# One list of evenly cut projection pieces for a whole attention program, v by halves, and the softmax sums in the accumulator's bank

## The chip, the cores and the metric

The kernel runs on one core of a Trainium2 chip. The metric is the time of one execution on the device in microseconds (us). The engines that matter are TensorE (PE, matrix products; its weight loads are shown apart as PEld), ScalarE (ACT, here only the exponential), VectorE (DVE), GpSimd (POOL) and the queue of SyncE (SP), which issues most transfers.

## What is computed

A batch of four images with 512 channels and 48x48 = 2304 positions goes through group normalisation, eight-head attention with a head size of 64, an output projection and a residual sum:

```python
hn = _group_norm(x, scale, bias)
qkv = jnp.einsum('oc,bchw->bohw', qkv_w, hn) + qkv_b[None, :, None, None]
qkv = qkv.reshape(b, 3, num_heads, d, t).astype(jnp.float16)
q, k, v = (qkv[:, 0], qkv[:, 1], qkv[:, 2])
scale = jnp.asarray(1.0 / math.sqrt(math.sqrt(d)), dtype=jnp.float16)
w = jnp.einsum('bhct,bhcs->bhts', q * scale, k * scale)
w = jax.nn.softmax(w, axis=-1)
a = jnp.einsum('bhts,bhcs->bhct', w, v).astype(jnp.float32)
a = a.reshape(b, c, hh, ww)
out = jnp.einsum('oc,bchw->bohw', proj_w, a) + proj_b[None, :, None, None]
return x + out
```

## The kernel before

`fast_path` does all the work here; `general_path` follows only if a flag says that some softmax sum left a safe range. Heads are taken in pairs: four batches of four pairs make 16 pairs `g` (`NG`). The 2304 query positions of a pair are cut into five blocks `j`, four of 512 and one of 256 (`QBLOCKS`). Keys come in 18 tiles of 128. A **step** (one entry of `stream`) handles three groups of two score tiles: six steps for a block of 512, three for the block of 256, 27 for a pair (`per_pair`), 432 in all.

In one step, `scores` (L784) multiplies k by q into one of three double banks `ps` of PSUM, and ScalarE takes the exponential of each into `p` (L803). One step later `values` (L806) multiplies v by `p` into the single accumulator bank `av`, and `add` (L841) sums the `p` tiles of the block on VectorE into `acc`. After the last step of a block VectorE copies `av` out (`avx`, L829). `add_up` (L855) multiplies `acc` by ones, which gives the softmax sums `sl`; VectorE copies them to `slx` (L872), a transfer puts them on partitions (`sums`), VectorE inverts them (L888), and two more transfers through DRAM (`row`, `ib`) spread the inverse; `divide` (L878) multiplies on GpSimd into `att`.

Beside the steps stands the **projection work** that feeds TensorE in between: q and k of later pairs (`qk_chain`, L641), v of the next batch (`v_chain`, L681), the output projection of the last batch (`proj_chain`, L730, with the weights split in a high and a low part), loading, statistics and normalisation of the next batch's x. A chain is a row of matmuls that ends in one bank; all chains, the group means and also `sl` use the one bank `pw` (`chain_bank`, L576), so a chain can start only when VectorE has emptied the one before. Chains are listed as pieces, one for each of the four channel chunks `c`, with an assumed length in us. Each batch has a list of its own (`beside[b]`); `fill` (L998) issues pieces until the batch's list is as far along as the batch's steps are. In the step in which `add_up` runs there is no `fill` (L1032 to L1035), since `sl` needs the bank `pw`; and the step before closes an open chain for the same reason.

The order on TensorE and VectorE is the order of the program; the other queues are ordered by the framework. Before the first step TensorE computes, with nothing beside it, q and k of pair 0 and all of v of batch 0 (L977 to L985): 10 chains for q and k, and 18 for v with 512 columns each. Behind the last step stands what is left of the last batch's projection, and the count of safe sums (L1040 to L1044).

Of the kernel before, what the change touches and what calls it, by code (L numbers as in the profile page):

```python
# [25 lines left out]
P = 128  # L26
# [439 lines left out]
def fast_path(  # L466
# [18 lines left out]
    apool = ctx.enter_context(tc.tile_pool(name="apool", bufs=6))  # L485
# [149 lines left out]
    def piece(us, run, first=False, last=False):  # L635
        return [us, run, first, last, 0, NG]
# [4 lines left out]
    def qk_chain(g, part, j):  # L641
# [4 lines left out]
        def one(c):  # L646
# [26 lines left out]
        return [  # L673
            piece(n / 600.0, lambda c=c: one(c), c == 0, c == NC - 1)
            for c in range(NC)
        ]
# [4 lines left out]
    def v_chain(b, i):  # L681
        pw = {}
        at = i * P % QB

        def one(c):
            if i == 0 and c == 0:
                vv[b] = [
                    vpool.tile(
                        [P, NT, C // 2], F16, tag=f"v{a}", bufs=1 + a, name=f"v{a}_{b}"
                    )  # L690
                    for a in range(2)
                ]
            if c == 0:
                pw[0] = chain_bank(f"pv_{b}_{i}")
            for lo in (0, D):
                nc.tensor.matmul(  # L696
                    pw[0][lo : lo + D, :],
                    hn[b, c, i * P // QB][:, at + lo : at + lo + D],
                    wqkv[:, c, 2 * C :],
                    start=(c == 0),  # L700
                    stop=(c == NC - 1),
                )
            if c == NC - 1:
                for half in range(2):
                    cols = bass.ts(half, C // 2)
                    nc.vector.tensor_tensor(  # L706
                        vv[b][half][:, i, :], pw[0][:, cols], bv[:, cols], ALU.add
                    )

        return [  # L710
            piece(0.86, lambda c=c: one(c), c == 0, c == NC - 1) for c in range(NC)
        ]
# [10 lines left out]
    def att32(b, j):  # L723
        o, n = QBLOCKS[j]
        t = work.tile([P, NC, QB], F32R, tag="a32", bufs=1, name=f"a32_{b}_{j}")
        for c in range(NC):
            nc.gpsimd.tensor_copy(t[:, c, :n], atts[b * NPAIR + c][:, o : o + n])  # L727
        at32[b, j] = t

    def proj_chain(b, j, m):  # L730
        o, n = QBLOCKS[j]
        ps = chain_bank(f"pr_{b}_{j}_{m}")
        for c in range(NC):
            for i, w in enumerate((whi, wlo)):
                nc.tensor.matmul(  # L735
                    ps[:, :n],
                    w[:, c, bass.ts(m, P)],
                    at32[b, j][:, c, :n],
                    start=(c == 0 and i == 0),
                    stop=(c == NC - 1 and i == 1),  # L740
                )
        xt = res.pop((b, j, m))
# [5 lines left out]
    def proj_block(b, j):  # L748

        pieces = []  # L750

        def ahead(k):
            if k < NQ * NC:
                pieces.append(piece(0.0, lambda: residual(b, k // NC, k % NC)))

        if j == 0:
            ahead(0)
            ahead(1)
        pieces.append(piece(0.0, lambda: att32(b, j)))
        for m in range(NC):  # L760
            ahead(j * NC + m + 2)
            pieces.append(
                piece(
                    QBLOCKS[j][1] / 290.0,
                    lambda m=m: proj_chain(b, j, m),
                    True,
                    True,
                )
            )
        return pieces  # L770
# [3 lines left out]
    av, acc, pts, avx, sums = {}, {}, {}, {}, {}  # L774
# [31 lines left out]
    def values(u):  # L806
# [3 lines left out]
        per = QB // n  # L810
        if k == 0:
            if j == 0:
                new_att(g)
            av[0] = ps_av.tile([P, QB], F32, tag="av", name=f"av_{g}_{j}")
        for r in range(BURST):
            for a in range(per):
                i = (k * BURST + r) * per + a
                for h in range(2):
# [3 lines left out]
                        vv[b][pr // 2][:, i, pr % 2 * P + lo : pr % 2 * P + lo + D],  # L822
                        pts[u][:, r, h, a * n : (a + 1) * n],
# [7 lines left out]
    def new_att(g):  # L831
        if g >= NG - 2:

            if g == NG - 2:
                spare = vpool.tile([P, 2, T], F16, tag="v1", bufs=2, name="att_last")
                for i in range(2):
                    atts[g + i] = spare[:, i, :]
        else:
            atts[g] = apool.tile([P, T], F16, tag="att", name=f"att_{g}")

    def add(u):  # L841

        g, j, k, _ = u
        pt = pts.pop(u)
        if k == 0:
            acc[g, j] = pt
            return
        before = acc[g, j]
        if k == 1:
            acc[g, j] = work.tile(  # L850
                [P, BURST, 2, QB], F16, tag="acc", bufs=1, name=f"acc_{g}_{j}"
            )
        nc.vector.tensor_tensor(acc[g, j], before, pt, ALU.add)  # L853

    def add_up(g, j):  # L855
        o, n = QBLOCKS[j]
        per = QB // n
        sl = chain_bank(f"sl_{g}_{j}")
        t = acc.pop((g, j))
        steps = [(r, a) for r in range(BURST) for a in range(per)]  # L860
        for r, a in steps:
            for h in range(2):
# [5 lines left out]
                    start=((r, a) == steps[0]),  # L868
                    stop=((r, a) == steps[-1]),
                )  # L870
        sx = work.tile([P, QB], F32, tag="rows", name=f"slx_{g}_{j}")
        nc.vector.tensor_copy(sx[:, :n], sl[:, :n])  # L872

        sums[g, j] = small.tile([P, 2, QB // P], F32, tag="sums", name=f"sums_{g}_{j}")
        for h in range(2):
            nc.sync.dma_start(sums[g, j][:, h, : n // P], sx[h * D : h * D + 1, :n])

    def divide(g, j):  # L878
        o, n = QBLOCKS[j]
        per = n // P  # L880
        sm = sums.pop((g, j))[:, :, :per]
        ok = fine[:, :, :per]
        for op, limit in ((ALU.is_ge, SUM_MIN), (ALU.is_le, SUM_MAX)):
            t = small.tile([P, 2, QB // P], F32, tag="in", name=f"in_{g}_{j}")
            nc.gpsimd.tensor_scalar(t[:, :, :per], sm, limit, None, op)  # L885
            nc.gpsimd.tensor_tensor(ok, ok, t[:, :, :per], ALU.mult)
        inv = small.tile([P, 2, QB // P], F32, tag="inv", name=f"inv_{g}_{j}")
        nc.vector.reciprocal(inv[:, :, :per], sm)  # L888
# [3 lines left out]
        )  # L892
        ib = work.tile([P, QB], F32, tag="rows", name=f"ib_{g}_{j}")
# [9 lines left out]
    beside = {b: [] for b in range(B)}  # L903

    def put(b, pieces, after=0, need=NG):
        for p in pieces:
            p[4], p[5] = after, need
        beside[b] += pieces

    def put_qk(b, g, parts, after=0):  # L910
        for part in parts:
            for j in range(NQ):
                put(b, qk_chain(g, part, j), after, g)

    for b in range(B):
        g = b * NPAIR
        if b == 0:
            for j in range(NQ):
                if j < NC:
                    put(b, [piece(0.0, lambda c=j: load_wproj(c))])  # L920
                if j > 0:
                    put(b, [piece(0.0, lambda c=j - 1: split_wproj(c))])
                for part in (1, 0):
                    put(b, qk_chain(g + 1, part, j), 0, g + 1)
        else:
            put_qk(b, g + 1, (0,))
        put_qk(b, g + 2, (1, 0))
        if b == B - 1:
            put(b, proj_block(b - 1, 0))
            put_qk(b, g + 3, (1, 0), per_pair - 1)  # L930
# [168 lines left out]
```

## Time and profile before

| | |
|---|---|
| time, median of 3 runs | 1798.94 us (1796.32 to 1800.29) |
| the profiled execution | 1798.37 us, of which its span is 1796.6 us |
| ScalarE busy | 1220.1 us, 68% of the span |
| VectorE busy | 1030.8 us, 57% |
| GpSimd busy | 334.7 us, 19% |
| moved to and from memory | 82.15 MB, mean 46 GB/s |

The span reaches from the first to the last instruction of the profiled execution; the 1.8 us around it are in the time and not in the profile. "Busy" is the time in which an engine had at least one instruction under way; the profile's ends of matmuls are modelled. In the views, L803 is line 803 of the kernel, `out<-in` are the program's names with the buffer numbers left out, and an arrow in brackets names what ended a wait.

### The profile page before, as it was taken

Reading aid. Unit: us, or ns where it says so; the run is one execution under the profiler, and the core shown is the slowest. Engines: PE = TensorE matmul, PEld = TensorE weight load, DVE = VectorE, ACT = ScalarE, POOL = GpSimd, SP = SyncE. Lnnn points to the kernel's source line nnn. Section 1 sums busy time; section 2 is a strip of 40 time slices with the busy share of each in tenths; the row PEclk is TensorE's granted clock in tenths of the full one; section 3 lists DMA queues with packets and bytes.
Section 4 is the critical chain, followed back from the end, with each engine's and each line's share of the span. In section 5 each row is a group of like instructions: output and inputs, shape, how many; then the busy total and the mean of one; then the engine's idle time right before and its main releaser. Section 6 shows DMA issues by size and latency. Waiting matters only on the chain. (4 is left out here: it accounts for less than half of the span.)

```text
span 1796.6 us, 26704 instructions
## 1 busy us (share of the span) xinstructions
PE 1652.7 (92%) x10706; PEld 649.1 (36%) x10706; DVE 1030.8 (57%) x1194; ACT 1220.1 (68%) x1297; POOL 334.7 (19%) x561
## 2 busy tenths in 40 slices
PE   4999997999999989899999998989999999999885
PEld 1333332333333343433333344343333334334443
DVE  5226557656555555756455555675555566666663
ACT  0027776677787775866677777685667888887971
POOL 1000122111121123210011113231011111222331
PEclk9999999999999999999999999999999999999998
DMA  5001022000000043310000014330000001104233
GB/s 194 0 1 31 19 50 78 10 13 13 10 14 16 17 112 118 90 39 13 10 13 16 13 40 122 107 92 13 13 10 13 14 15 23 53 16 132 61 107 110
DMA packets 90406, 82.15 MB, mean 46 GB/s; under 512 B 51488, under 2 KB 58144, under 8 KB 90272
## 3 DMA queue, kind: packets, MB, share of 16 engines
q1 hardware_dynamic: 83712, 62.75, 12.9%
q0 software_dynamic: 4592, 14.18, 2.7%
q10 hardware_dynamic: 1968, 3.41, 0.6%
q8 instruction: 86, 1.41, 0.3%
q14 instruction: 48, 0.39, 0.1%
HBM read 60.83 MB, written 19.17 MB: 45 GB/s over the span
## 5 line engine op out<-in xcount | busy, mean ns | idle before, releaser
L803 ACT ACTIVATE p<-ps 128x1024 f16<-128x1024 f32 x1296 | 1218.8, 1038 | 523.6 <-PE ps L796 523.4
L655 PE MATMUL pqk<-x,wqkv 128*64 128x512 f32 (+1 forms) x2560 | 530.4, 551 | 6.4 <-DVE x L628 4.4
L853 DVE TENSOR_TENSOR acc<-acc,p 128x3072 f16<-128x3072 f16 x272 | 482.3, 1773 | 31.0 <-ACT p L803 29.5
L796 PE MATMUL ps<-q,k 64*128 64x512 f16 (+1 forms) x2880 | 388.2, 360 | 64.0 <-ACT p L803 63.1
L820 PE MATMUL av<-p,v 128*64 128x512 f16 (+1 forms) x2880 | 363.7, 366 | 0.6 <-DVE avx L829 0.6
L655 PEld LDWEIGHTS pqk<-x,wqkv 128*64 128x64 f32 x2560 | 179.4, 137 | 255.3 <-issue 196.7
L796 PEld LDWEIGHTS <-k 64*128 64x128 f16 x2880 | 119.3, 94 | 412.3 <-issue 366.9
L696 PE MATMUL pv<-wqkv,x 128*64 128x512 f32 x1152 | 260.7, 599 | 4.3 <-DVE x L628 4.3
L885 POOL TENSOR_SCALAR in<-sums 128x8 f32<-128x8 f32 (+1 forms) x160 | 55.1, 345 | 964.3 <-DMA sums<-slx 957.9
L820 PEld LDWEIGHTS <-v 128*64 128x64 f16 x2880 | 125.6, 109 | 188.9 <-issue 149.6
L898 POOL TENSOR_TENSOR att<-avx,ib 128x512 f16<-128x512 f32 (+1 forms) x70 | 105.6, 1508 | 303.4 <-DMA ib<-row 275.9
L853 DVE TENSOR_TENSOR acc<-p,p 128x3072 f16<-128x3072 f16 x80 | 145.1, 1814 | 24.8 <-ACT p L803 24.7
L735 PE MATMUL pr<-a,whi 128*128 128x512 f32 (+1 forms) x320 | 126.1, 401 | 19.2 <-DVE r L743 10.3
L706 DVE TENSOR_TENSOR v<-pv,bv 128x256 f16<-128x256 f32 x144 | 54.4, 420 | 144.1 <-PE pv L696 144.0
L696 PEld LDWEIGHTS pv<-wqkv,x 128*64 128x64 f32 x1152 | 81.3, 138 | 148.2 <-issue 131.3
L664 DVE TENSOR_SCALAR k<-pqk,bqkv 128x512 f16<-128x512 f32 (+1 forms) x80 | 55.7, 696 | 109.4 <-PE pqk L655 109.4
L735 PE MATMUL pr<-a,wlo 128*128 128x512 f32 (+1 forms) x320 | 117.6, 374 | 0.0
L664 DVE TENSOR_SCALAR q<-pqk,bqkv 128x512 f16<-128x512 f32 (+1 forms) x80 | 55.6, 696 | 105.1 <-PE pqk L655 105.1
L829 DVE COPY avx<-av 128x512 f32<-128x512 f32 (+1 forms) x80 | 51.0, 637 | 92.9 <-PE av L820 92.0
L872 DVE COPY slx<-sl 128x512 f32<-128x512 f32 (+1 forms) x80 | 51.0, 637 | 86.2 <-PE sl L864 85.9
L743 DVE SCALAR_TENSOR_TENSOR r<-pr,bproj,r 128x512 f32<-128x512 f32 (+1 forms) x80 | 55.4, 693 | 47.6 <-PE pr L735 37.8
L735 PEld LDWEIGHTS pr<-a,whi 128*128 128x128 f32 x320 | 60.1, 188 | 59.1 <-issue 19.5
(48 smaller groups left out, 456.3 us busy)
## 6 DMA issues: line engine op xcount, KB each, us to landing
r<-x_dram SPq DMA_DIRECT2D x64, 256.0 KB, 2.9
ib<-row SPq DMA_DIRECT2D x128, 128.0 KB, 3.1
out_dram<-r SPq DMA_DIRECT2D x64, 256.0 KB, 3.0
x<-x_dram POOLq DMA_DIRECT2D x48, 256.0 KB, 3.3
x<-x_dram ACTq DMA_DIRECT2D x8, 256.0 KB, 7.0
x<-x_dram SPq DMA_DIRECT2D x8, 256.0 KB, 7.0
wqkv<-qkv_wT_dram SPq DMA_DIRECT2D x2, 1024.0 KB, 8.2
sums<-slx SPq DMA_DIRECT2D x128, 2.0 KB, 2.0
```

The source lines that it names most:

```text
L655: nc.tensor.matmul(pw[0][lo : lo + D, :n], wqkv[:, c, w0 + lo : w0 + lo + D], hn[b, c, j], start=(c == 0), stop=(c == NC - 1),)
L664: nc.vector.tensor_scalar(qk[g][part][:, o : o + n], pw[0][:, :n], bqkv[:, col : col + 1], SCALE, ALU.add, ALU.mult,)
L696: nc.tensor.matmul(pw[0][lo : lo + D, :], hn[b, c, i * P // QB][:, at + lo : at + lo + D], wqkv[:, c, 2 * C :], start=(c == 0), stop=(c == ...
L706: nc.vector.tensor_tensor(vv[b][half][:, i, :], pw[0][:, cols], bv[:, cols], ALU.add)
L735: nc.tensor.matmul(ps[:, :n], w[:, c, bass.ts(m, P)], at32[b, j][:, c, :n], start=(c == 0 and i == 0), stop=(c == NC - 1 and i == 1),)
L743: nc.vector.scalar_tensor_tensor(xt, ps[:, :n], bproj[:, m : m + 1], xt, ALU.add, ALU.add)
L796: nc.tensor.matmul(ps[:, h, a * n : (a + 1) * n], kt[rows, bass.ts(i, P)], qt[rows, o : o + n], start=True, stop=True,)
L803: nc.scalar.activation(pt[:, r], ps, AF.Exp)
L820: nc.tensor.matmul(av[0][lo : lo + D, :n], vv[b][pr // 2][:, i, pr % 2 * P + lo : pr % 2 * P + lo + D], pts[u][:, r, h, a * n : (a + 1) * ...
L853: nc.vector.tensor_tensor(acc[g, j], before, pt, ALU.add)
L885: nc.gpsimd.tensor_scalar(t[:, :, :per], sm, limit, None, op)
L898: nc.gpsimd.tensor_tensor(atts[g][:, o : o + n], avx.pop((g, j))[:, :n], ib[:, :n], ALU.mult)
```

## The change

1. **One list, even pieces.** The lists by batch become one list `beside` for the program. A chain of four chunks with 512 columns is cut in two halves (`HALVES`), one of 256 columns is a single piece (`WHOLE`), and the projection's blocks of 256 columns go two chains to a bank (`proj_pieces`), so that nearly every piece is 1.7 us by the list's own figures. `fill` works with a credit: each step adds the rate that the list needs to meet the next due time, and a piece is issued where the credit covers half of it. Work is put in another order within the list, with a `gap` of steps before some statistics.
2. **v by halves.** `v_chain` computes 256 of v's 512 columns for two position tiles, side by side in one bank. The first half (pairs 0 and 1 of a batch) is due before the batch, the second half within the batch. So nine v chains stand before the first step, not 18.
3. **Sums in the accumulator's bank.** `add_up` takes its bank from the pool of `av`, is issued at the start of a step, ahead of the scores, and that step has a `fill` too, between the scores and the values. `add` now stands ahead of `values`, so that the copy `avx` follows the sum.
4. **Division in three steps.** `check_sums` and `invert` run one step before `divide`.
5. **The last two blocks** (`direct`: pair 15, j 3 and 4) invert the sums on VectorE and multiply there, with no way through DRAM; `att32` converts their part on VectorE, and their last `p` goes into `add_up` directly and not through `add`.
6. x of the next batch is loaded through SP's queue, not through GpSimd's; `apool` has 8 buffers (before 6), v's second half has one buffer (before two).

```diff
-    def v_chain(b, i):
+    def v_chain(b, half, i):
...
-            for lo in (0, D):
-                nc.tensor.matmul(
-                    pw[0][lo : lo + D, :],
-                    hn[b, c, i * P // QB][:, at + lo : at + lo + D],
-                    wqkv[:, c, 2 * C :],
...
+            at = (i + a) * P % QB
+            for c in range(NC):
+                for lo in (0, D):
+                    nc.tensor.matmul(
+                        pw[0][lo : lo + D, a, :],
+                        hn[b, c, i * P // QB][:, at + lo : at + lo + D],
+                        wqkv[:, c, 2 * C + half * C // 2 :][:, : C // 2],
...
     def add_up(g, j):
...
-        sl = chain_bank(f"sl_{g}_{j}")
+        sl = ps_av.tile([P, QB], F32, tag="av", name=f"sl_{g}_{j}")
...
+        if direct(g, j):
+            source = rows() if n == QB else sl
+            inv = work.tile([P, QB], F32, tag="rows", name=f"inv_{g}_{j}")
+            nc.vector.reciprocal(inv[:, :n], source[:, :n])
+            nc.vector.tensor_tensor(
+                atts[g][:, o : o + n], avx.pop((g, j))[:, :n], inv[:, :n], ALU.mult
+            )
...
+    def put_v(b, half):
+        for i in range(0, NT, 2):
+            if half == 0 and i % 4 == 2 and i // 4 + 1 < NQ:
+                put_run(norm, b, i // 4 + 1)
+            g = b * NPAIR + 2 * half
+            put(v_chain(b, half, i), (g - 2) * per_pair + 1, g)
...
-    for i in range(NT):
-        for p in v_chain(0, i):
+    for i in range(0, NT, 2):
+        for p in v_chain(0, 0, i):
             p[1]()
...
+    def fill(n):
+        rate, work = 0.0, 0.0
+        for us, _, _, _, _, _, need in beside:
+            work += us
+            left = min(need * per_pair, len(stream)) - n
+            rate = max(rate, work / max(left, 1))
+        credit[0] = min(credit[0] + rate, 4.0)
         ended = False
...
+            us, _, first, last, gap, after, _ = beside[0]
+            if after > n or n < issued[0] + gap or (first and ended):
                 break
...
+            if credit[0] < us / 2:
                 break
+            issue(n)
             ended = ended or last
...
+    for n in range(end):
         if ended(n - 2):
             add_up(*stream[n - 2][:2])
+        wanted(stream[n][0], n)
+        scores(stream[n])
+        if n > 0:
+            add(stream[n - 1])
+        if ended(n - 2):
+            fill(n)
+        if n > 0:
+            values(stream[n - 1])
+        if ended(n - 3):
+            check_sums(*stream[n - 3][:2])
+            if not direct(*stream[n - 3][:2]):
+                invert(*stream[n - 3][:2])
+        if ended(n - 4):
+            divide(*stream[n - 4][:2])
+        if not ended(n - 2):
+            fill(n)
```

How the order moves is seen at three places. On TensorE, around the sums of the first block of pair 0, before (`ps_1_1_2` is the third score tile of the second step of block 1, `pqk` a chain for q or k; the weight loads between the matmuls and rows of the same tile are left out):

```order
L820 MATMUL av_0_574<-p_0_5_669,v_0_336 64x512
...
L655 MATMUL pqk_0_1_689<-x_2_1_108,wqkv 64x512 x2
L655 MATMUL pqk_0_1_689<-x_3_1_110,wqkv 64x512 x2
...
L796 MATMUL ps_1_1_2_730<-q_222,k_223 128x512
...
L820 MATMUL av_1_734<-p_1_0_694,v_0_336 64x512
...
L864 MATMUL sl_0_741<-acc_0_603,ones_162 64x512
...
L796 MATMUL ps_1_2_0_754<-q_222,k_223 128x512
```

The same place now:

```order
L856 MATMUL av_0_535<-p_0_5_632,v_0_336 64x512
...
L672 MATMUL pqk_0_1_652<-x_2_1_108,wqkv 64x512 x2
L672 MATMUL pqk_0_1_652<-x_3_1_110,wqkv 64x512 x2
L904 MATMUL sl_0_684<-acc_0_560,ones_162 64x512
...
L831 MATMUL ps_1_1_2_705<-q_222,k_223 128x512
L672 MATMUL pqk_1_2_713<-x_0_2_112,wqkv 64x512 x2
L672 MATMUL pqk_1_2_713<-x_1_2_114,wqkv 64x512 x2
L856 MATMUL av_1_718<-p_1_0_657,v_0_336 64x512
```

The sums `sl` now stand one step earlier, directly behind the half chain of the step before, and half a chain stands in their own step, where there was none.

On VectorE at the end of that block, before (`acc` rows are `add`; the `q` row empties the chain's bank):

```order
L853 TENSOR_TENSOR acc_0_603<-acc_0_603,p_0_4_639 128x3072
L829 COPY avx_0_713<-av_0_574 128x512
L853 TENSOR_TENSOR acc_0_603<-acc_0_603,p_0_5_669 128x3072
L664 TENSOR_SCALAR q_551<-pqk_0_1_689,bqkv 128x512
L872 COPY slx_0_748<-sl_0_741 128x512
```

And now:

```order
L888 TENSOR_TENSOR acc_0_560<-acc_0_560,p_0_4_602 128x3072
L888 TENSOR_TENSOR acc_0_560<-acc_0_560,p_0_5_632 128x3072
L865 COPY avx_0_677<-av_0_535 128x512
L681 TENSOR_SCALAR q_514<-pqk_0_1_652,bqkv 128x512
L914 COPY slx_0_691<-sl_0_684 128x512
```

The copy `avx` has moved behind the last sum of the block, and `sl`, which takes the bank that `avx` empties, has to wait for both.

On TensorE before the first step, where v of batch 0 begins, before:

```order
L696 MATMUL pv_0_338<-wqkv,x_0_0_96 64x512 x2
L696 MATMUL pv_0_338<-wqkv,x_1_0_98 64x512 x2
L696 MATMUL pv_0_338<-wqkv,x_2_0_100 64x512 x2
L696 MATMUL pv_0_338<-wqkv,x_3_0_102 64x512 x2
L696 MATMUL pv_1_349<-wqkv,x_0_0_96 64x512 x2
```

And now:

```order
L712 MATMUL pv_0_0_337<-wqkv,x_0_0_96 64x256 x2
L712 MATMUL pv_0_0_337<-wqkv,x_1_0_98 64x256 x2
L712 MATMUL pv_0_0_337<-wqkv,x_2_0_100 64x256 x2
L712 MATMUL pv_0_0_337<-wqkv,x_3_0_102 64x256 x2
L712 MATMUL pv_0_2_355<-wqkv,x_0_0_96 64x256 x2
```

A chain now holds 16 matmuls of 256 columns (the four rows stand twice in it, for two position tiles) in place of eight of 512.

Counted over the whole program in the same order (a chunk of 512 columns is a quarter of a chain; a chain of 256 columns or of the projection is one piece):

| steps by what stands beside them | before | now |
|---|---|---|
| empty, with the sums `sl` | 79 | 2 |
| empty or a group mean only, no sums | 23 | 21 |
| a quarter of a chain | 40 | 0 |
| half a chain or one piece | 135 | 350 |
| three quarters or a whole chain | 154 | 58 |

(That is 431 steps; the last one, with all that follows it, is left out.) Of the 23 steps that hold no chain now, 14 lie in pair 15 and five in pair 2.

More of the change, by code (lines that the diff above doesn't have):

```diff
@@ L867, in add_up @@
                     t[:, r, h, a * n : (a + 1) * n],
-                    start=((r, a) == steps[0]),
-                    stop=((r, a) == steps[-1]),
-                )
[L871 to L882, printed above, removed]
+                    start=(i == 0),
@@ L982, in fast_path @@
                 p[1]()
[L983 to L984 removed]
+    for i in range(0, NT, 2):
+        for p in v_chain(0, 0, i):
             p[1]()
     alone[0] = False
[L988 to L1003 removed]
+    issued = [0]
@@ L1040, in fast_path @@
+    alone[0] = True
+    add(stream[-1])
+    values(stream[-1])
+    att32(B - 1, NQ - 1, range(NC - 1))
+    add_up(NG - 1, NQ - 1)
+    att32(B - 1, NQ - 1, (NC - 1,))
+    while beside:
+        issue(end)
+    check_sums(NG - 1, NQ - 1)
+    for pieces in projs[B - 1, NQ - 1][1]:
+        for p in pieces:
+            p[1]()
     good = small.tile([P, 1], F32, tag="good", bufs=1, name="good")
```

375 lines of the change are left out of this document (211 added, 164 removed).

## The prediction

> **What bounds the kernel now.** I read the page first, then the busy time by stretch, the waits, and the timeline of single steps.
>
> ```profile
> span 1796.6 us, 26704 instructions
> PE 1652.7 (92%) x10706; PEld 649.1 (36%) x10706; DVE 1030.8 (57%) x1194; ACT 1220.1 (68%) x1297; POOL 334.7 (19%) x561
> ```
>
> ```profile
> 0.00:45.00 45.00, 20.18 (x86) 7.19 (x88) 24.04 (x52) 1.28 (x1) 6.68 (x18) 1.00 0.60 193
> 90.00:135.00 45.00, 43.97 (x224) 13.96 (x220) 12.57 (x25) 11.56 (x13) 0.00 (x0) 1.00 0.00 1
> 270.00:315.00 45.00, 35.74 (x232) 12.80 (x230) 33.51 (x50) 28.74 (x31) 10.74 (x22) 0.94 0.28 77
> 1665.00:1710.00 45.00, 37.29 (x286) 18.29 (x285) 29.05 (x28) 42.00 (x46) 17.16 (x23) 1.00 0.23 62
> 1755.00:1800.00 45.00, 20.84 (x138) 15.15 (x134) 11.71 (x19) 4.50 (x5) 7.49 (x18) 0.83 0.33 101
> ```
>
> The first column after the length is TensorE's busy time, the fourth ScalarE's, then comes the granted clock. TensorE is busy 92% of the span and ScalarE 68%: TensorE's work, and the time that TensorE loses, make the span. The loss has three places: the load at the start (20.18 busy of 45), the end (20.84 of 45), and some 97 us between 135 and 1755 (1796.6 less 1652.7 is 144, less 25 at the start, 1 up to 135 and 21 at the end). What it waits for:
>
> ```profile
> PE ps L796 <- ACT p L803: 63.1, 140, 0.5
> PE gmean L596 <- DVE mv L594: 30.0, 4, 19.6
> PE pr L735 <- DVE r L743: 10.3, 10, 3.2
> PE pr L735 <- POOL a L727: 8.8, 7, 3.0
> PE pv L696 <- DVE x L628: 4.3, 2, 2.2
> ```
>
> Most of it is 140 short waits of the scores for ScalarE to free a bank `ps`. A busy engine and a waiting one at once mean uneven steps, and the timeline shows both kinds:
>
> ```profile
> 1223.47 0.77 PE av L820 x6
> 1224.24 3.43 PE pv L696 x16
> 1227.67 0.75 PE ps L796 x6
> 1228.43 0.77 PE av L820 x6
> ```
>
> ```profile
> 1229.03 3.60 PE L696 MATMUL pv<-wqkv,x 128*64 128x512 f32 x16
> 1233.99 0.81 PE L864 MATMUL sl<-acc,ones 128*64 128x512 f16 x6
> 1235.90 0.39 PE L796 MATMUL ps<-q,k 64*128 64x512 f16 x2 [0.53 <-ACT p L803]
> 1236.89 3.60 PE L696 MATMUL pv<-wqkv,x 128*64 128x512 f32 x16
> ...
> 1700.13 0.39 PE L796 MATMUL ps<-q,k 64*128 64x512 f16 x2 [0.52 <-ACT p L803]
> 1702.88 0.39 PE L796 MATMUL ps<-q,k 64*128 64x512 f16 x2 [0.53 <-ACT p L803]
> ...
> 1562.98 1.02 PE L655 MATMUL pqk<-x,wqkv 128*64 128x512 f32 x4
> 1565.73 1.88 PE L655 MATMUL pqk<-x,wqkv 128*64 128x512 f32 x8
> ```
>
> A step with a whole v chain repeats after 1228.43 - 1223.47 = 4.96 us, of which 3.43 are the chain: scores and values take **1.53 us**. With the sums step between them, two chains start 7.86 us apart, so that step took 7.86 - 4.96 = 2.90. An empty step takes 2.75, ScalarE's own pace for three tiles; the step with a quarter chain too (1562.98 to 1565.73). So a step is ScalarE's below about 2.8 us of TensorE work and TensorE's above it, and half a chain (1.53 + 1.72 = 3.25) is enough.
>
> **The change, part by part.** The matmuls stay the same but for v's width and some more `sl` at the very end, and the v that leaves the start (nine chains) comes back beside the steps. So I price what TensorE loses.
>
> *Even pieces.* Losses before, with the counts of steps given with the change: 79 sums steps lose 2.90 - 1.53 - 0.75 = 0.62 (0.75 of the 0.81 busy us lie before the next scores), 49 us; 23 empty ones lose 2.75 - 1.53 = 1.22, 28 us; 40 with a quarter lose 2.75 - 1.53 - 0.86 = 0.36, 14 us: 91 in all. Now: 21 at 1.22 and 2 at 0.62, 27 us; the other 408 hold 1.7 us or more and are TensorE's. That is 64 less. By the row of waits alone (63.1, in the same proportion 27/91) it would be 44 less, since the waits leave out what the broken-up matmuls lose. I take **-57**, with 44 and 64 as ends. The cover this rests on is ScalarE's slack: 3.25 less 2.8 us in each step.
>
> *v by halves.* The price is in the rows of chains for q and k that are 256 wide, and in the stretch before the steps, where nothing is beside them:
>
> ```profile
> 55.13 3.16 PEld L655 LDWEIGHTS pqk<-x,wqkv 128*64 128x64 f32 x30 [0.29 <-issue]
> 57.08 0.48 DVE L664 TENSOR_SCALAR k<-pqk,bqkv 128x256 f16<-128x256 f32 x1 [0.98 <-PE pqk L655]
> 58.59 61.97 PE L696 MATMUL pv<-wqkv,x 128*64 128x512 f32 x288
> 58.80 0.48 DVE L664 TENSOR_SCALAR q<-pqk,bqkv 128x256 f16<-128x256 f32 x1 [1.24 <-PE pqk L655]
> ...
> L655 PE MATMUL pqk<-x,wqkv 128*64 128x256 f32 x512 | 61.1, 380 | 2.0 <-DVE k L664 2.0
> L696 PE MATMUL pv<-wqkv,x 128*64 128x512 f32 x1152 | 260.7, 599 | 4.3 <-DVE x L628 4.3
> ```
>
> 18 v chains took 61.97 us, 3.44 each. Two 256-wide chains of eight matmul pairs were emptied 58.80 - 57.08 = 1.72 us apart, half of 3.44 for half the columns. So the narrower matmul costs **0**. The other end: by busy time, 61.1/256 is 0.239 us a pair and 260.7/576 is 0.453; 1152 pairs of the one less 576 of the other are +14. That busy time counts the ends of many broken chains, so I take 0.
>
> [...]
>
> *Sums in `av`'s bank.* On TensorE `sl` now stands ahead of the scores, the half chain and the values; all of them, and so ScalarE, wait where it waits. It waits for `acc` and `avx`:
>
> ```profile
> L853 DVE TENSOR_TENSOR acc<-acc,p 128x3072 f16<-128x3072 f16 x272 | 482.3, 1773 | 31.0 <-ACT p L803 29.5
> L664 DVE TENSOR_SCALAR k<-pqk,bqkv 128x512 f16<-128x512 f32 x64 | 48.0, 750 | 103.5 <-PE pqk L655 103.5
> L829 DVE COPY avx<-av 128x512 f32<-128x512 f32 x64 | 44.2, 691 | 82.9 <-PE av L820 82.9
> ```
>
> From the end of the chain piece of the step before the last values, VectorE has an eviction (0.75, in 48 of 80 blocks by the order), the sum 1.77 and the copy 0.69: 3.21 us; TensorE has scores, values and half a chain, 3.25. It is nearly even: some 0.1 us each, and in three blocks a normalisation of four tiles stands in the way (about 2 us each). I take **+8**; ends 0 and 48 x 0.75 = +36, if one more eviction always stands ahead. Behind `sl`, its own copy of 0.69 is covered by the scores and the half chain (2.5 us) before the next block's values.
>
> *Statistics and the rest.* Four `gmean` waits of 30.0 us less the one at the start (19.6) are 10.4; the gaps give VectorE its steps: **-6** (0 to -10). The projection's waits, 10.3 + 8.8: its pieces are now one to a step throughout, the three residual buffers stay: **-4** (0 to -8). Moving x to SP's queue, division over three steps and `apool` lie beside TensorE's work: 0; if SP's queue were held up, `inv` on VectorE would be late and count above.
>
> *The end.* From the last scores on:
>
> ```profile
> 1755.65 0.63 PE L796 MATMUL ps<-q,k 64*128 64x256 f16 x8
> 1776.68 2.79 SPq L746 DMA_DIRECT2D out_dram<-r  x2
> 1784.42 0.48 DVE L743 SCALAR_TENSOR_TENSOR r<-pr,bproj,r 128x256 f32<-128x256 f32 x1 [0.45 <-DMA r<-x_dram]
> 1785.26 0.14 DVE L1044 TENSOR_SCALAR flag<-count 1x1 int32<-1x1 f32 x1 [0.28 <-PE count L1043]
> ```
>
> The last residual sum starts 28.8 us after them and the span ends 11.3 us after the flag. The same ten chains stand there now. The direct blocks spare the way through DRAM, but what paces this stretch is the residual tiles, three buffers that go out and come in again (the last sum waits for `r<-x_dram`), and these stay. So **-3** (+3 to -10). What an inversion of 512 columns on VectorE takes no row shows: the rows of 8 and 4 columns are 203 and 178 ns, so between a plain copy's 0.69 and some 3.4 us (an estimate, 6.2 ns a column); it is done twice and delays nothing for longer than that.
>
> ```profile
> L888 DVE RECIPROCAL inv<-sums 128x8 f32<-128x8 f32 x64 | 13.0, 203 | 77.3 <-DMA sums<-slx 77.3
> L888 DVE RECIPROCAL inv<-sums 128x4 f32<-128x4 f32 x16 | 2.8, 178 | 15.8 <-DMA sums<-slx 15.7
> ```
>
> Sum: -57 + 0 + 8 - 6 - 4 - 3 = -62. From the profiled execution's 1798.4 that gives 1736; the median of the runs is 0.6 higher, so **1737**.
>
> **Rivals.**
> 1. *Less of the loss goes.* The waits for ScalarE shrink only by the row's 44, and `sl` stands behind VectorE at its dear end, +36 and not +8: 1737 + 13 + 28 = 1778; with one of the two, 1750 to 1765. For it speaks how evenly the two engines meet at a block's end; against it that VectorE is busy only 57%.
> 2. *More goes.* All terms at their good ends: -64 - 10 - 8 - 10 = -92, so 1707. The clock speaks for it: it was 0.94 in the stretch with 9 us of waits, so fewer waits give some clock back.
> 3. *It does not do what it says*: the pieces are even in the list's own figures, but another engine sets the steps and nothing is gained. At 3.25 us a step ScalarE has 0.4 us of slack and VectorE's sum and eviction take 2.5, so I see no such engine; 1799.
> 4. *Slower: the weight loads of v show.* There are 576 more pairs of loads. If each held the matmuls up by its 0.14 us (a load's mean is 137 to 138 ns), this is 81 us: 1737 + 81 = 1818. It decides from 62/576 = 0.11 us a pair on. Against it stand the two chains 1.72 us apart, with the same loads and the same width.
>
> ```profile
> L696 PEld LDWEIGHTS pv<-wqkv,x 128*64 128x64 f32 x1152 | 81.3, 138 | 148.2 <-issue 131.3
> ```
>
> **How the numbers follow.** The forecast (1720 to 1750) has a chance of 0.60, rival 1 0.20, rival 2 0.12, rival 3 0.04, rival 4 0.04. Leaving out 2 in 10 means the far half of rival 2, the dear end of rival 1 and rivals 3 and 4: 1713 to 1768. A measurement of this kernel can tell about 0.2% (3.6 us) from no change. Faster by more than that are the forecast and rivals 1 and 2, 0.92; slower is rival 4 and a part of rival 3, 0.05; 0.03 remain.
>
> **What would show it.** The waits of the scores for ScalarE fall from 63 to about 20 us, nearly all of them in pair 15. The first exponential comes some 31 us earlier, and full stretches of 45 us have TensorE busy over 44 with ScalarE near 36. v chains before the first step stay at 3.44 us each; if they take 4.5, rival 4 is right. Waits of `sl` for VectorE stay near 8 us in total; 36 would be rival 1. The flag comes some 26 us after the last scores. The forecast is wrong if steps with one piece do not take 3.2 to 3.3 us.

## The result, and the profile after

| | before | after |
|---|---|---|
| time, median | 1798.79 us (1796.32 to 1800.29, 4 runs) | 1709.11 us (1707.22 to 1710.66, 4 runs) |
| span of the profiled execution | 1796.6 us | 1706.4 us |
| ratio | | 0.9502, 95% interval 0.9486 to 0.9519 |

The kernel became 5.0% faster, 89.7 us; the forecast was 62 us, and its range ended 4 us above the result. The page after, its first two lines:

```profile
span 1706.4 us, 28896 instructions
PE 1631.4 (96%) x11876; PEld 719.9 (42%) x11876; DVE 1019.8 (60%) x1124; ACT 1232.9 (72%) x1297; POOL 345.0 (20%) x497
```

TensorE's idle time fell from 143.9 us to 75.0, and its busy time by 21.3. The waits of TensorE after (total in us, times, longest):

```profile
PE gmean L596 <- DVE mv L594: 22.7, 4, 20.1
PE ps L831 <- ACT p L838: 14.9, 33, 0.5
PE sl L904 <- DVE avx L865: 12.8, 10, 2.7
...
PE pr L760 <- POOL a L752: 3.3, 2, 2.6
...
PE pv L712 <- DVE x L628: 1.4, 1, 1.4
PE pr L760 <- DVE r L771: 0.5, 1, 0.5
```

The scores' waits for ScalarE went from 63.1 us to 14.9 (11.7 of them in pair 15), those of the projection from 19.1 to 3.8. New are 12.8 us in which ten of the 80 sums wait for the copy of the accumulator; seven of these waits, 9.4 us, lie where the next batch's statistics and normalisation run (300 to 365, 640 to 765 and 1080 to 1220 us). The matmuls of the scores, by groups (busy us, mean ns of one; idle us before them), before and then after:

```profile
L796 PE MATMUL ps<-q,k 64*128 64x512 f16 (+1 forms) x2880 | 388.2, 360 | 64.0 <-ACT p L803 63.1
```

```profile
L831 PE MATMUL ps<-q,k 64*128 64x512 f16 (+1 forms) x2880 | 364.4, 360 | 15.3 <-ACT p L838 14.9
```

The same 2880 matmuls with the same mean take 24 us less busy time: by the records their single times (2880 times 360 ns, 1037 us) lie over one another, and they filled 364.4 us with 14.9 us of waits between them where they filled 388.2 with 63.1. The row of waits alone misses this part.

By stretches of 45 us after (length; busy time of TensorE, its weight loads, VectorE, ScalarE, GpSimd; granted clock, DMA share, GB/s):

```profile
45.00:90.00 45.00, 45.00 (x372) 25.75 (x369) 10.97 (x19) 0.02 (x1) 0.00 (x0) 1.00 0.00 1
180.00:225.00 45.00, 45.00 (x370) 20.10 (x368) 25.56 (x26) 36.80 (x40) 10.70 (x16) 1.00 0.09 16
315.00:360.00 45.00, 37.31 (x284) 16.32 (x286) 37.01 (x57) 31.82 (x35) 7.55 (x12) 0.92 0.14 35
1665.00:1710.00 45.00, 28.02 (x204) 20.42 (x200) 18.96 (x25) 8.24 (x9) 6.76 (x15) 0.90 0.33 104
```

In 21 of the 38 such stretches of the whole program TensorE is never idle while ScalarE is busy for 32.8 to 36.9 us of the 45; the forecast was near 36. The stretch of batch 1's statistics and normalisation (315 to 360) is the one bad place left between the start and 600 us. The timeline of single steps and of the end:

```profile
58.37 31.25 PE L712 MATMUL pv<-wqkv,x 128*64 128x256 f32 x288
89.54 0.61 PE L831 MATMUL ps<-q,k 64*128 64x512 f16 x4
...
203.42 0.82 PE L831 MATMUL ps<-q,k 64*128 64x512 f16 x6
...
206.67 0.82 PE L831 MATMUL ps<-q,k 64*128 64x512 f16 x6
...
1673.01 0.83 PE L831 MATMUL ps<-q,k 64*128 64x256 f16 x12
...
1699.78 0.15 DVE L1163 TENSOR_SCALAR flag<-count 1x1 int32<-1x1 f32 x1 [0.28 <-PE count L1162]
```

A step with one piece takes 206.67 - 203.42 = 3.25 us. The nine v chains before the first step take 31.25 us, 3.47 each. The first scores come 30.9 us earlier (120.48 before, from the same view), and the flag 26.8 us after the last scores (29.6 before). The span ends 6.6 us after the flag; before it was 11.3.

Put together, with the start and the moved v left out, the 1635.2 us from the first to the last scores became 1583.5 although 31.25 us of v came in: **83 us less lost**, and 7.6 less at the end.

### The profile page after: what moved, and what is told of

It reads as the page before. It is cut to its first block, busy times and chain, and to the rows that moved or that the text cites. A ratio compares the mean times of both kernels' runs of the same rounds, so it can differ in the third digit from the quotient of the medians.

```text
span 1706.4 us, 28896 instructions
## 1 busy us (share of the span) xinstructions
PE 1631.4 (96%) x11876; PEld 719.9 (42%) x11876; DVE 1019.8 (60%) x1124; ACT 1232.9 (72%) x1297; POOL 345.0 (20%) x497
## 4 chain that ended last, share of the span: by engine, by line
PE 87%; DVE 5%; DMA 3%; ACT 3%; issue 2%; POOL 0%; SPq 0%; DVEq 0%; POOLq 0%; ACTq 0%
PE pqk L672 29%; PE ps L831 17%; PE av L856 17%; PE pv L712 14%; PE pr L760 7%; PE sl L904 3%; ACT p L838 3%; DVE acc L888 2%; DVE st L589 1%; DMA out_dram<-r 1%; DMA x<-x_dram 1%; DMA r<-x_dram 1%; DVE x L628 1%; DVE avx L865 0%; DMA ib<-row 0%
## 5 line engine op out<-in xcount | busy, mean ns | idle before, releaser
L838 ACT ACTIVATE p<-ps 128x1024 f16<-128x1024 f32 x1296 | 1231.6, 1027 | 427.5 <-PE ps L831 426.9
L831 PE MATMUL ps<-q,k 64*128 64x512 f16 (+1 forms) x2880 | 364.4, 360 | 15.3 <-ACT p L838 14.9
L941 POOL TENSOR_SCALAR in<-sums 128x8 f32<-128x8 f32 (+1 forms) x160 | 115.0, 719 | 803.0 <-DMA sums<-slx 796.5
L712 PE MATMUL pv<-wqkv,x 128*64 128x256 f32 x2304 | 267.7, 380 | 1.4 <-DVE x L628 1.4
L831 PEld LDWEIGHTS <-k 64*128 64x128 f16 x2880 | 107.7, 94 | 291.6 <-issue 245.4
L963 POOL TENSOR_TENSOR att<-avx,ib 128x512 f16<-128x512 f32 (+1 forms) x78 | 119.8, 1536 | 421.5 <-DMA ib<-row 378.2
L712 PEld LDWEIGHTS pv<-wqkv,x 128*64 128x64 f32 x2304 | 160.0, 137 | 93.9 <-issue 7.2
L720 DVE TENSOR_TENSOR v<-pv,bv 128x512 f16<-128x512 f32 x72 | 49.8, 691 | 135.5 <-PE pv L712 135.5
L752 POOL CAST a<-att 128x512 fp32r<-128x512 f16 (+1 forms) x75 | 64.3, 891 | 88.0 <-PE pr L760 87.7
L904 PE MATMUL sl<-acc,ones 128*64 128x512 f16 (+1 forms) x576 | 67.4, 350 | 13.0 <-DVE avx L865 12.8
```

Source lines behind the costliest of these rows:

```text
L712: nc.tensor.matmul(pw[0][lo : lo + D, a, :], hn[b, c, i * P // QB][:, at + lo : at + lo + D], wqkv[:, c, 2 * C + half * C // 2 :][:, : C / ...
L752: engine.tensor_copy(at32[b, j][:, c, :n], atts[b * NPAIR + c][:, o : o + n])
L831: nc.tensor.matmul(ps[:, h, a * n : (a + 1) * n], kt[rows, bass.ts(i, P)], qt[rows, o : o + n], start=True, stop=True,)
L838: nc.scalar.activation(pt[:, r], ps, AF.Exp)
L904: nc.tensor.matmul(sl[lo : lo + D, :n], ones16, t[:, r, h, a * n : (a + 1) * n], start=(i == 0), stop=(i == len(steps) - 1),)
L941: nc.gpsimd.tensor_scalar(t, sm, limit, None, op)
```

## The experiments

Times are medians and are compared with the changed kernel's 1709.11. The kernel before ran beside each group of experiments, and its median lay between 1799.9 and 1804.0 there; so a difference of a few us between groups is read from the ratios to it (0.001 is 1.8 us), or from the traces.

**Whole chains.** Does the evenness matter, or only the new bank, list and division?

```diff
-        return chain_pieces(n / 600.0, one, HALVES if n == QB else WHOLE)
+        return chain_pieces(n / 600.0, one, WHOLE)
...
-        return chain_pieces(1.72, one, (range(1), range(1, 2)))
+        return chain_pieces(1.72, one, (range(2),))
```

> The changed kernel with every chain as one piece of 3.44 us (no halves); all else as changed. By the step sum (a step takes the larger of TensorE's work and about 2.8 us) the order has 154 empty steps in place of 23, so 170 us are lost where the changed kernel loses 26: 1709 + 144 = 1853 us, slower than the kernel before, and the waits of the scores for ScalarE rise from 14.9 to over 100 us. The rival, that the gain came from the earlier first exponential, the sums' bank and the other queue, and not from evenness, expects at most some 20 us more than 1709.

Measured: 1893.0 us (1890.8 to 1895.2), ratio to before 1.0507 (1.0468 to 1.0547). Its waits, and the scores' group:

```profile
PE ps L831 <- ACT p L838: 122.9, 245, 0.5
PE sl L904 <- DVE avx L865: 44.8, 30, 2.7
```

```profile
L831 PE MATMUL ps<-q,k 64*128 64x512 f16 (+1 forms) x2880 | 400.3, 359 | 123.3 <-ACT p L838 122.9 <-DVE v L720 0.3
```

So without the even cut the changed kernel is slower than the kernel before. By the order of its matmuls it has 106 more empty steps and 25 more sums steps without a piece; at the prediction's 1.22 and 0.62 us that is 145. The rows give the same: 122.9 - 14.9 = 108 of waits and 36 of busy time (its scores are busy for 400.3 us), 144 together, as expected. The time is 40 us above the expected 1853, and these 40 are mostly the sums, whose wait for VectorE rose by 32. The price of an uneven step holds; that uneven steps also bring back waits at the sums was not in it.

**Quarters.** The same question with the smallest edit: chains of q and k in four pieces of 0.86 us.

```diff
-    HALVES = (range(NC // 2), range(NC // 2, NC))
+    HALVES = tuple(range(c, c + 1) for c in range(NC))
```

> Chains of 512 columns for q and k are cut in quarters of 0.86 us and not in halves; all else as in the changed kernel. By the count of steps 52 steps then hold one quarter and are ScalarE's, 19 us more are lost by the prediction's price: 1725 to 1731, and the waits of the scores for ScalarE rise from 14.9 to 30 or more. Rival: the size of a piece does not matter as long as the rate is even: 1707 to 1711.

Measured: 1729.06 us (1725.6 to 1734.6), ratio 0.9611 (0.9591 to 0.9631).

```profile
PE ps L831 <- ACT p L838: 31.3, 80, 0.5
```

```profile
L831 PE MATMUL ps<-q,k 64*128 64x512 f16 (+1 forms) x2880 | 372.1, 360 | 31.8 <-ACT p L838 31.3
```

20 us more where 52 steps at 0.36 are 19. This is the cleanest test of the price: nothing else in the rows grew by more than 3 us. Of the 24 us that the scores' rows grew, a third (364.4 to 372.1) is again busy time and not waiting.

**The sums step left empty.** The sums keep the accumulator's bank, but no piece is issued in that step.

```diff
         if n > 0:
             add(stream[n - 1])
-        if ended(n - 2):
-            fill(n)
```

> The changed kernel without the piece in the sums step (its bank stays the accumulator's). By the step sum 97 steps are empty in place of 23, 119 us lost in place of 26: 1709 + 93 = 1802 us. By the price that the prediction put on an empty sums step (0.62 us, 79 of them) it would be 1709 + 49 = 1758. If the sums' new bank were the gain by itself, it stays near 1709.

Measured: 1831.84 us, ratio 1.0168 (1.0130 to 1.0205).

```profile
PE ps L831 <- ACT p L838: 77.0, 163, 0.5
...
PE av L856 <- DVE slx L914: 13.3, 10, 2.4
PE pqk L672 <- DVE q L681: 7.7, 9, 0.9
PE pqk L672 <- DVE k L681: 7.3, 11, 0.9
```

Both expected times were too low, and the kernel is slower than the one before: the bank alone gains nothing, it pays only with a piece in that step. The scores' rows account for 84 of the 123 us (62 of waits, 22 of busy time); 74 more empty steps at 1.22 us are 90, at 0.62 us 46, so the dearer price is the one that fits here. Some 13 us more are values that wait for the sums' copy, which the piece used to cover, and another 13 are chains for q and k that wait for VectorE to empty the one before. Nearly all of the latter lie in two places, where the list has fallen so far behind that nine chains stand in one step, and ScalarE stands still beside them:

```profile
945.74 2.85 ACT L838 ACTIVATE p<-ps 128x1024 f16<-128x1024 f32 x3 [34.67 <-PE ps L831]
```

So part of the loss is a list that was not made anew for fewer steps; what such a list would lose was not tried. The rest of the 123, some 13, I could not place.

**The copy ahead of the sum.** VectorE's order in a block's last step turned round: the accumulator is copied out before the last `p` is added. (In the step of the sums the piece now stands ahead of `add` too.)

```diff
-        if n > 0:
-            add(stream[n - 1])
...
-            values(stream[n - 1])
+            values(stream[n - 1], False)
+            add(stream[n - 1])
```

> The changed kernel with values ahead of add again, so that the copy avx stands ahead of the block's last sum on VectorE. sl then waits for the sum and no longer for the copy; both have to be done before it, so the 12.8 us of its waits stay about as they are: 1709 within 3 us. The rival, that the copy behind the sum is what costs them, expects 5 to 10 us less.

Measured: 1761.68 us, ratio 0.9782 (0.9752 to 0.9813): some 50 us slower, so both expectations were wrong. Its waits and the timeline around one block's end, then the same place in the changed kernel:

```profile
PE sl L904 <- DVE acc L888: 55.0, 70, 2.5
```

```profile
212.54 0.69 DVE L865 COPY avx<-av 128x512 f32<-128x512 f32 x1 [2.68 <-PE av L856]
213.15 1.75 DVE L888 TENSOR_TENSOR acc<-acc,p 128x3072 f16<-128x3072 f16 x1
...
214.96 0.84 PE L904 MATMUL sl<-acc,ones 128*64 128x512 f16 x6 [0.80 <-DVE acc L888]
```

```profile
206.74 1.76 DVE L888 TENSOR_TENSOR acc<-acc,p 128x3072 f16<-128x3072 f16 x1 [1.05 <-ACT p L838]
...
208.42 0.68 DVE L865 COPY avx<-av 128x512 f32<-128x512 f32 x1
...
209.82 0.81 PE L904 MATMUL sl<-acc,ones 128*64 128x512 f16 x6
```

With the copy first, the 1.75 us sum stands behind a copy that waits for TensorE's values, though its own input from ScalarE was there 2.3 us before (the exponentials of that step end at 210.88). 70 of 80 sums then wait 0.79 us each. That is 42 of the some 50 us; TensorE's busy time grew by 9 more. `add` ahead of `values` is worth more than the sums' whole price.

**The sums behind the scores.** Do the 12.8 us at the sums hold up the scores?

```diff
+        wanted(stream[n][0], n)
+        scores(stream[n])
         if ended(n - 2):
             add_up(*stream[n - 2][:2])
-        wanted(stream[n][0], n)
-        scores(stream[n])
```

> The sums of a block stand behind the scores of their step and not ahead of them; all else as in the changed kernel. Theory that the 12.8 us in which the sums wait for the copy of the accumulator hold up the scores, and so ScalarE: these waits fall to under 6, time 1700 to 1705. Rival: that wait is only moved, since the scores have then to wait for ScalarE and the values behind the sums wait for their copy: 1707 to 1711.

Measured: 1703.69 us (1700.8 to 1706.7), ratio 0.9470 (0.9456 to 0.9484).

```profile
PE ps L831 <- ACT p L838: 15.3, 34, 0.5
PE sl L904 <- DVE avx L865: 5.3, 6, 1.5
...
PE av L856 <- DVE slx L914: 3.4, 3, 2.1
```

They do, in good part: 7.5 us of the sums' waits go, 3.4 come back as values that wait for the sums' copy, and the scores wait no longer than before. So about half of what the sums' new place costs can be had back.

**The projection.** Three runs ask why its waits went from 19.1 to 3.8 us. Between the first and the last scores, those for the residual sums went from 10.3 to 0 and those for GpSimd's conversion from 3.4 to 2.6; the others lie behind the last scores. In the first run, x of the next batch is loaded through GpSimd's queue again.

```diff
-            put_run(load_x, b + 1, j, (nc.sync,))
+            put_run(load_x, b + 1, j, (nc.gpsimd,))
```

> The changed kernel with x of the next batch loaded through GpSimd's queue, as before. The prediction put this edit at nothing: 1709 within 3 us. The rival: GpSimd, which stood 78 us waiting to issue these loads, was what held the projection back (its waits fell from 19.1 to 3.8 us, forecast was 4 less): then 1709 + 8 to 12 us, with the waits of the projection for GpSimd's conversions and for the residual sums back.

Measured: 1715.04 us (1712.5 to 1715.7), ratio 0.9516 (0.9489 to 0.9544). The projection's waits stayed (4.0 and 0.8 us), so this queue did not cause them. Yet it is 5.9 us slower by the medians, 2.5 by the ratios (whose intervals overlap), and its profiled span 6.6 us longer. The row of GpSimd's queue and the flag:

```profile
q0 software_dynamic: 4592, 14.18, 2.8%
```

```profile
1702.14 0.14 DVE L1163 TENSOR_SCALAR flag<-count 1x1 int32<-1x1 f32 x1 [0.28 <-PE count L1162]
```

The flag is 2.4 us later, and the span ends at 1713.0, 10.9 us after it and not 6.6. The converse, the kernel before with x through SP's queue:

```diff
-            put(b, [piece(0.0, lambda b=b, j=j: load_x(b + 1, j, (nc.gpsimd,)))])
+            put(b, [piece(0.0, lambda b=b, j=j: load_x(b + 1, j, (nc.sync,)))])
```

> The kernel before with only x of the next batch moved to SP's queue. The prediction's price for this is nothing: 1799 within 3 us. The rival (GpSimd's queue held the projection back) expects 8 to 12 us less, 1787 to 1791, with the projection's waits for GpSimd and for the residual sums gone.

Measured: 1795.64 us (10 runs), ratio 0.9976 (0.9963 to 0.9989), which is 2 to 7 us faster, with 16.7 us of projection waits, near the 19.1 before. Its span of 1793.2 ends 7.0 us after its flag at 1786.2, not 11.3. All twelve kernels with x on SP's queue end 6.5 to 7.0 us after the flag, the two with x on GpSimd's 10.9 and 11.3: **some 4.3 us behind the flag hang on that queue**. What fills them stands in the view of the line whose `with` closes the program (count; shortest, middle and longest in ns; first and last start), in the kernel before and then in the changed one:

```profile
L1095 POOLq DRAIN  x3: 52/107/5376, 1790.4 to 1796.3; - x3
```

```profile
L1214 POOLq DRAIN  x3: 52/106/476, 1704.4 to 1706.1; - x3
```

GpSimd's longest `DRAIN`, an instruction that the kernel's text does not hold, takes 5.38 us in the kernel before, with x on GpSimd's queue, and 0.48 us in the changed one.

In the second, the last batch's chains for q come ahead of batch 2's projection, and not between its blocks, to leave work for pair 15.

```diff
+            put_qk(g + 3, 0)
             for j in range(NQ):
-                put_qk(g + 3, 0, (j,))
                 put_proj(old, j)
```

> The changed kernel with the third batch's projection behind all q chains of the last batch in the list, so that seven of the 14 empty steps of pair 15 get a piece. By the step sum 17 us are lost in place of 26: 1709 - 9 = 1700 us, with the scores' waits for ScalarE near 9 us. The rival: the end is set by the residual tiles and the last batch's projection, and what pair 15 gains is lost in the end: within 2 us of 1709.

Measured: 1710.39 us, ratio 0.9497 (0.9470 to 0.9523).

```profile
PE pr L760 <- POOL a L752: 11.6, 8, 3.3
PE ps L831 <- ACT p L838: 9.0, 20, 0.5
```

Six us of the scores' waits go and eight come back: a block's projection now follows its conversion at once and waits for GpSimd. So in the changed kernel it is the q chain between conversion and projection that hides the conversion. (Another 3.2 us of this profile are the first chain of the program, which waits 5.8 us for its x and not 2.6; this wait lies before the edit's place and is 2.6 to 6.5 us in the profiles of all these kernels.) The third run keeps that place and converts ahead, into the buffers of x that are free by then:

```diff
+            at32[b, j] = [
+                xpool.tile([P, n], F32R, tag=f"x{c}_{j}", name=f"a32_{b}_{j}_{c}")
+                for c in range(NC)
+            ]
...
             for j in range(NQ):
                 put_qk(g + 3, 0, (j,))
+                put_convert(old, j)
+            for j in range(NQ):
                 put_proj(old, j)
```

> Batch 2's output projection stands behind the q chains of the last batch, as in the run with the late projection, but its five blocks are converted ahead into the buffers of x, which are free by then, so that no chain waits for GpSimd's conversion. Count of steps: 7 empty steps in the last pair and not 14, 9 us less. If the waits for the conversion (11.6 us in the run with the late projection) ate that gain: waits of the scores for ScalarE near 9 us, of the projection for the conversion under 3, time 1698 to 1703. Rival: what comes free is lost at another place whatever the conversion does: 1707 to 1711.

Measured: 1704.21 us (1702.2 to 1706.6), ratio 0.9472 (0.9458 to 0.9486).

```profile
PE ps L841 <- ACT p L848: 9.0, 20, 0.5
...
PE pr L770 <- POOL a L762: 3.1, 1, 3.1
```

With the conversion out of the way the gain stays, if smaller than the 9 us of the step count. None of the three runs touches what removed the 10.3 us of waits for the residual sums.

**The end and the start.** The last two blocks divided through DRAM like the others (with all that hangs on `direct`: their conversion goes back to GpSimd, their last `p` to `add`):

```diff
-        return g == NG - 1 and j >= NQ - 2
+        return False
...
+    divide(NG - 1, NQ - 2)
     add_up(NG - 1, NQ - 1)
+    check_sums(NG - 1, NQ - 1)
+    invert(NG - 1, NQ - 1)
+    divide(NG - 1, NQ - 1)
...
-    check_sums(NG - 1, NQ - 1)
```

> The changed kernel with the last two blocks divided through DRAM like all others. The stretch from the last scores' start to the end is 33.4 us in the changed kernel and 41 before, where the prediction put it 3 shorter. If the direct division is what shortened it, this run is 4 to 8 us slower (1713 to 1717) with the stretch back near 40. If the residual tiles' way out and in again sets it, as the prediction had it, the time stays within 2 us of 1709.

Measured: 1714.47 us (1711.3 to 1715.3), ratio 0.9516 (0.9488 to 0.9544). The last scores and the flag:

```profile
1675.17 0.83 PE L831 MATMUL ps<-q,k 64*128 64x256 f16 x12
...
1706.20 0.14 DVE L1166 TENSOR_SCALAR flag<-count 1x1 int32<-1x1 f32 x1 [0.28 <-PE count L1165]
```

The flag comes 6.4 us later, but 2.2 of them lie ahead of the last scores, where the first chain's wait alone was 3.7 us longer in this profile (6.3 us, not 2.6). The stretch from the last scores to the flag is 31.0 us in place of 26.8. So by the trace the direct division is worth 4.3 us, by the medians 5.4, by the ratios 2.5, and these intervals overlap: its sign is likely, its size not settled. Both halves of v of batch 0 ahead of the first step:

```diff
-        put_v(b, 1)
+        if b > 0:
+            put_v(b, 1)
...
-        for p in v_chain(0, 0, i):
-            p[1]()
+        for half in range(2):
+            for p in v_chain(0, half, i):
+                p[1]()
```

> The changed kernel with both halves of v of batch 0 ahead of the first step, as before (18 chains, 62 us, in place of 31). By the step sum the work only moves: 93.4 + 1537 against 62.5 + 1569 us, so 1709 within 3 us. The rival, that the earlier first exponential shortens the span because ScalarE's row is the one that ends last, expects up to 31 us more, 1740.

Measured: 1710.67 us, ratio 0.9497 (0.9471 to 0.9523). Where v stands makes no difference by itself.

**Both improvements**, the conversion ahead and the sums behind the scores:

> The projection converted ahead into x's buffers and the sums behind the scores, together. If both take off what is expected of each: 1690 to 1698. If only the first does: 1698 to 1703; if neither: 1707 to 1711.

Measured: 1704.48 us (1700.5 to 1705.3), ratio 0.9465 (0.9451 to 0.9480). They do not add up. Its profile shows 5.0 us in which the projection waits for its residual sums, where the two runs had 0.9 and 1.7; why was not tried. (The 6.5 us that its first chain waits at the start are no part of the edits.) Each of the three gives about 1704, 5 us below the changed kernel. The interval of the conversion ahead touches the changed kernel's at 0.9486; the other two end just below it, at 0.9484 and 0.9480. So a gain of some 5 us is likely, and for the conversion not certain.

## Why the prediction was wrong

The mechanism was the forecast one, and "more goes" (rival 2, 1707, given 0.12) is what came. (The clock, which rival 2 had speak for it, hardly moved: the mean granted clock was 0.991 before and is 0.993 now; with whole chains, where the scores wait 122.9 us for ScalarE, it was 0.994, so it did not go by these waits.) The step that failed is the sizing of the sum:

| term | forecast | measured |
|---|---|---|
| even pieces | -57 (-44 to -64) | about -72: waits 63.1 to 14.9, scores' busy time 388.2 to 364.4 |
| v by halves | 0 | 0: 3.47 us a chain, not 3.44 |
| sums in `av`'s bank | +8 | about +9: 12.8 us of waits, 4.0 before (five rows) |
| statistics, normalisation | -6 | about -11: group means within the stream 10.4 to 2.6, v for x 4.3 to 1.4 |
| projection's waits in the stream | -4 | about -11: residual sums 10.3 to 0, conversion 3.4 to 2.6 (the other 5.5 of the 19.1 lay behind the last scores) |
| x through SP's queue | 0 | about -4, behind the flag |
| the end, up to the flag | -3 | -2.8 |

The last column adds up to -92, where 89.7 us were measured.

- **"I take -57, with 44 and 64 as ends."** This is the largest miss, 15 of the 28 us. The count of steps gave 64, and the quarters and whole chains bear out its prices (19 forecast and 20 found; 145 and 144 in the scores' rows). The 44 came from the row of waits, which leaves out what broken-up matmuls lose, as the prediction itself said. So 44 was not an end of the range but a part of the sum, and a value between the two had no ground. Of the 8 us beyond 64 no run tells the cause.
- **"The projection's waits: -4."** A row of 19 us that the change reorders was priced at a fifth. What went is the 10.3 us for the residual sums (1.6 us came back as chains for q and k that wait for them). That one piece to a step removes them was not tried alone, nor was the new order of the list, so the cause stays open. The run with the late projection shows only what keeps the small wait for the conversion small.
- **"x to SP's queue ... lie beside TensorE's work: 0."** The transfers do; the 4.3 us behind the flag do not. The question could have been raised before: the prediction notes 11.3 us between the flag and the span's end, and 5.38 of them are GpSimd's `DRAIN`.
- **The statistics: -6.** Their waits went by 11, past the good end of 10. No run varied their place and gaps, the division over three steps or the numbers of buffers; the rows show that the waits went, and not which of these edits took them.
- **v** came as forecast. The doubled loads, which rival 4 priced at 81 us, do not show: a chain takes 3.47 us, and from 45 to 90 us 25.75 us of loads lie in a stretch with 45.00 of 45 us of matmuls.
- **The sums and the end** came out near the forecast sizes, in part by luck. The prediction's parts for the sums, 0.1 us in each block and 2 in three of them, would make 14 and not 8 over 80 blocks; found are ten waits and none at the 70 other sums. At the end it had the residual tiles set the pace; by the trace the direct division shortens that stretch by 4.3 us.
- **The range** left out the far half of rival 2. Three terms went past their good ends together (72, 11 and 11 us against 64, 10 and 8). They may share a reason, even steps and so fewer waits everywhere; that was not shown.

## What to carry to other kernels

Where two engines take turns in steps, price each kind of step by its cadence and count the steps; the row of waits is a lower bound (the loss was a third to a half above it here), since the matmuls that waits broke up also lost time as "busy" (the scores' 388.2 us with 63.1 of waits, 364.4 with 14.9). When work is cut to size, look at every step that cannot take a piece: a bank given up for the sums was worth nothing until a piece could stand beside them. Read the order on the engine that closes a block: the same two VectorE instructions turned round cost some 50 us here. And look at what stands behind the kernel's own last instruction: here it was up to 11.3 us, and some 4.3 of them could be saved.

## What was not expected of the hardware

- Loads of 14 MB through GpSimd's queue during the run made the span end some 4.3 us later after the flag (11.3 us and not 7.0 with the kernel before, 10.9 and not 6.6 with the changed one). GpSimd's longest `DRAIN` took 5.38 us in the kernel before and 0.48 in the changed one, though the last of these loads was issued at 1170.0 us in the kernel before.
- After a wait of 2.66 us among short steps, TensorE ran at about half speed for some 6 us:

```profile
325.05 0.84 PE L856 MATMUL av<-p,v 128*64 128x512 f16 x6
328.55 1.49 PE L904 MATMUL sl<-acc,ones 128*64 128x512 f16 x6 [2.66 <-DVE avx L865]
329.97 1.46 PE L831 MATMUL ps<-q,k 64*128 64x512 f16 x6
331.51 1.49 PE L856 MATMUL av<-p,v 128*64 128x512 f16 x6
332.94 1.31 PE L831 MATMUL ps<-q,k 64*128 64x512 f16 x6
334.18 0.84 PE L856 MATMUL av<-p,v 128*64 128x512 f16 x6
```

```profile
327.20:333.90 6.70, 5.27 (x24) 1.61 (x23) 5.97 (x12) 3.39 (x5) 0.00 (x0) 0.50 0.02 1
```

The granted clock from 327.2 to 333.9 us is 0.50. In the run with the sums behind the scores the like came after a wait of 2.13 us: two groups of six matmuls behind it took 1.46 and 1.49 us and not 0.82 and 0.84. Yet a wait of 2.81 us in the kernel before (up to 1109.15) left the clock at 1.00 (from 1109.2 to 1114.0), so in these runs the length of the one wait does not decide it; what does was not tried. In this place a wait of 2.7 us costs some 5 us: four groups of matmuls take 5.75 us together in place of 3.32.
- The inversion that no row before showed:

```profile
1670.30 3.35 DVE L925 RECIPROCAL inv<-slx 128x512 f32<-128x512 f32 x1
```

3.35 us for 512 columns, near the estimate of 3.4 and five times a copy of the same size (0.68 us).
